# A four-layer graph network in one launch: layer 0's layernorm passes on GpSimd, its first row logits loaded early, layer 1's bias row added on VectorE

## The chip, the cores and the metric

The kernel runs on one core of a Trainium2 chip. The metric is the device time of one execution in microseconds (us). The kernel before takes 4507.97 us (median of three runs, 4505.92 to 4508.1); the profiled execution has a span of 4498.9 us from its first to its last instruction, and the profile's numbers are from that one.

A core has five engines with their own instruction streams, each working through its stream in order: TensorE (PE in the profile, and PEld for its weight loads), VectorE (DVE), ScalarE (ACT), GpSimd (POOL) and SyncE (SP, which here only issues transfers). They work in parallel and wait for one another by semaphores. Data moves between memory and the on-chip buffers by DMA.

## The reference

N is 4096 nodes, D is 256 features. Four layers follow one another, each with a residual and a layernorm:

```python
x = _layernorm(x + _L0_gnn_ref(x, W, b, a, adj))       # 8-head attention on the graph
x = _layernorm(x + _L1_gnn_ref(x, adj, weight, bias))  # (diag(adj) + adj) @ (x @ w) + bias
x = _layernorm(x + _L2_gnn_ref(x, adj, ...))           # top-p attention diffusion, two steps
x = _layernorm(x + _L3_gnn_ref(x, adj, W, b))          # mean aggregation, relu

def _L0_gnn_ref(x, W, b, a, adj_matrix):
    node_feats = (x @ W.T + b).reshape(num_nodes, num_heads, half)
    logit_parent = (node_feats * a[None, :, :half]).sum(axis=-1)
    logit_child = (node_feats * a[None, :, half:]).sum(axis=-1)
    attn_logits = leaky_relu(logit_parent[:, None, :] + logit_child[None, :, :], 0.2)
    attn_logits = where(abs(adj_matrix)[..., None] != 0.0, attn_logits, 0.0)
    attn_probs = softmax(attn_logits, axis=1)
    return einsum('ijh,jhc->ihc', attn_probs, node_feats)

def _L1_gnn_ref(x, adj, weight, bias):
    support = x @ weight
    return (diagonal(adj) + adj) @ support + bias      # the diagonal is added to every row
```

(The bodies of layers 2 and 3 are left out: the change does not touch them.)

## The kernel before

Layer 0 has two stages. `sums0` computes the node features and logits and, by dense matmuls over the whole adjacency, the sums that do not depend on the sign of a logit; it also writes a one-byte copy of the adjacency (`nad`), the row logits (`lpd`), the sums (`zd`) and the matmul operands (`gmd`) to memory. Then `layer0` goes through two halves of four heads each, and in each half through four tiles of 1024 rows. For each head it makes masks (logit sum above zero, and an edge), 32 column blocks of them in groups of four, partly on VectorE and partly on ScalarE, and multiplies them with `gm`. In half 1 it adds the residual and normalises.

```python
def moments(self, pool, src):                                   # cut
    for q in range(n):
        nc.vector.bn_stats(stats[:, q, :], src[:, q, :])        # L80
        nc.vector.bn_aggr(mv[:, q, :], stats[:, q, :])          # L81
    var = pool.tile([P, n], F32, name="ln_var")
    nc.gpsimd.tensor_scalar_add(var, mv[:, :, 1], EPS)          # L83
    nc.gpsimd.tensor_tensor(rstd, var, self.power..., ALU.pow)  # L84
    return mv, rstd

def layernorm(self, pool, dst, src):
    mv, rstd = self.moments(pool, src)
    for q in range(src.shape[1]):                               # L91
        self.nc.vector.tensor_scalar(dst[:, q, :], src[:, q, :], mv[:, q, 0:1], rstd[:, q:q + 1],
                                     op0=ALU.subtract, op1=ALU.mult)

def layer0(self):                                               # cut; Q = 8, NB = 32, K = 4, H = 8
    ...
    self.sums0(both, nlc, fac, lpd, nad, zd, gmd)
    self.open_x()
    self.load1()                                                # layer 1's weight and bias, on ScalarE's queue
    ...
    work = ctx.enter_context(tc.tile_pool(name="l0w", bufs=2))
    for half in range(2):
        for it in range(N // IT):
            i0 = it * Q
            ...                                                 # loads of na, and of gm at it == 0
            if half:
                nc.sync.dma_start(X[:, i0:i0 + Q, :], xr[:, i0:i0 + Q, :])
                y0 = work.tile([P, Q, D // 2], F32, name="y0", bufs=1)
                nc.sync.dma_start(y0, yd[i0:i0 + Q].rearrange("b p d -> p b d"))
            y = work.tile([P, Q, H // 2, C], F32, name="y")
            for hh in range(H // 2):
                h = half * (H // 2) + hh
                lpb = work.tile([P, IT], F32, name="lpb")
                nc.gpsimd.dma_start(lpb, bass.AP(tensor=lpd.tensor, ...))          # L243
                z = work.tile([P, Q, C1], F32, name="z")
                nc.gpsimd.dma_start(z, zd[i0:i0 + Q, :, h]...)                     # L246
                for g in range(NB // K):
                    ...
                    if g % 8 in (2, 5, 7):
                        for k in range(K):                                         # L257
                            nc.vector.tensor_scalar(sg[:, k, :], lpb, nlc[:, jc, h:h + 1], 2.0 ** -5, ...)
                        nc.vector.tensor_tensor(*bits, ALU.bitwise_and)            # L259
                    else:
                        for k in range(K):                                         # L264
                            nc.scalar.activation(sg[:, k, :], lpb, AF.Sign, scale=-1.0, ...)
                        nc.vector.scalar_tensor_tensor(bits[0], bits[1], ...)      # L266
                    ...                                                            # 32 matmuls, L272
                ...                                       # reduction of acc (L277), scaling, y of this head
            if not half:
                nc.gpsimd.dma_start(yd[i0:i0 + Q]..., y)
                continue
            for q in range(0, Q, 2):
                xs = X[:, i0 + q:i0 + q + 2, :]
                nc.vector.tensor_add(xs[:, :, :D // 2], xs[:, :, :D // 2], y0[:, q:q + 2])   # L296
                nc.vector.tensor_add(xs[:, :, D // 2:], xs[:, :, D // 2:], y[:, q:q + 2])    # L297
                self.layernorm(work, xs, xs)

def sums0(self, both, nlc, fac, lpd, nad, zd, gmd):             # cut
    ...                                                         # loads of w0, b0, a0
    for t, cs in ((w0, (0, 1)), (b0, (0,))):
        for c in cs:
            for s in range(2):
                prod = work.tile([P, H, C], F32, name="prod")
                nc.vector.tensor_mul(prod, t[:, c, :D]..., a_bc[:, s])                        # L375
                nc.vector.tensor_reduce(t[:, c, D + s * H:D + (s + 1) * H], prod, AX.X, ALU.add)  # L376
    ...                                                         # features and logits, support matmuls at L401
    self.factors0(wp, ps, both, nlc, fac)
    with nc.allow_non_contiguous_dma(reason="the diagonal"):
        nc.scalar.dma_start(self.diag, bass.AP(tensor=self.adjt.tensor, ...))                 # L432
    ...                                                         # the dense sums, matmuls at L479

def layer1(self):                                               # cut
    dg = pool.tile([P, NB], F32R, name="dg")
    nc.vector.tensor_copy(dg, self.diag)                        # L665
    ...                                                         # x @ w1, split into two parts, in XD
    ...                                                         # row = diagonal @ support + bias
    for b in range(NB):
        ps = psum.tile([P, 512], F32, name="ps_adj")            # psum has bufs=2
        ...                                                     # 32 matmuls into ps, L695
        xb = X[:, b:b + 1, :]
        nc.gpsimd.tensor_add(xb[:, 0], xb[:, 0], row)           # L700
        nc.vector.tensor_add(xb[:, 0], xb[:, 0], ps[:, :D])     # L701
        nc.vector.tensor_add(xb[:, 0], xb[:, 0], ps[:, D:])     # L702
        self.layernorm(work, xb, xb)
```

A tile scheduler sets the order of the instructions on each engine within a priority that follows the program, so instructions of a later part can be issued among those of an earlier one.

Of the kernel before, what the change touches and what calls it, by code (L numbers as in the profile page):

```python
# [9 lines left out]
F32 = mybir.dt.float32  # L10
I32 = mybir.dt.int32
F32R = mybir.dt.float32r
# [5 lines left out]
ALU = mybir.AluOpType  # L18
# [4 lines left out]
P = 128  # L23
# [28 lines left out]
class Net:  # L52
# [9 lines left out]
    def constants(self):  # L62
        nc = self.nc
        pool = self.ctx.enter_context(self.tc.tile_pool(name="const", bufs=1))
        self.ident = pool.tile([P, P], F32, name="ident")
        make_identity(nc, self.ident)
        self.power = pool.tile([P, 1], F32, name="power")
        nc.vector.memset(self.power, -0.5)
        self.deg = pool.tile([P, self.NB], F32, name="deg")
        self.diag = pool.tile([P, self.NB], F32, name="diag")  # L70

    def moments(self, pool, src):
# [13 lines left out]

    def layernorm(self, pool, dst, src):

        mv, rstd = self.moments(pool, src)
        for q in range(src.shape[1]):  # L90
            self.nc.vector.tensor_scalar(dst[:, q, :], src[:, q, :], mv[:, q, 0:1], rstd[:, q:q + 1],  # L91
                                         op0=ALU.subtract, op1=ALU.mult)

# [99 lines left out]
    def layer0(self):  # L193
        nc, tc, NB, D, N = self.nc, self.tc, self.NB, self.D, self.N
        H, C = 8, 32
        C1 = C + 1
        IT = min(1024, N)
        Q = IT // P
        keep = self.ctx.enter_context(tc.tile_pool(name="l0k", bufs=1, space=DRAM))
        self.fits = keep.tile([1, 1], I32, name="fits")  # L200
        with ExitStack() as ctx:
            pool = ctx.enter_context(tc.tile_pool(name="l0", bufs=1))
            dram = ctx.enter_context(tc.tile_pool(name="l0d", bufs=1, space=DRAM))

            both = pool.tile([P, NB, 2, H], F32, name="both")
            lp, lc = both[:, :, 0, :], both[:, :, 1, :]
            nlc = pool.tile([P, NB, H], F32, name="nlc")

            fac = pool.tile([P, 4, NB, H], F32, name="fac")
            lpd = dram.tile([H, N], F32, name="lpd")  # L210


            nad = self.nad
            zd = dram.tile([NB, P, H, C1], F32, name="zd")
            yd = dram.tile([NB, P, D // 2], F32, name="yd")
            gmd = dram.tile([2, P, NB, H // 2, 6 * C1], BF16, name="gmd")
            self.sums0(both, nlc, fac, lpd, nad, zd, gmd)

# [7 lines left out]
            gm = gp.tile([P, NB, H // 2, 6 * C1], BF16, name="gm")  # L226
            na = gp.tile([P, NB, IT], U8, name="na")
            for half in range(2):
                for it in range(N // IT):
# [10 lines left out]
                    for hh in range(H // 2):  # L240
                        h = half * (H // 2) + hh
                        lpb = work.tile([P, IT], F32, name="lpb")
                        nc.gpsimd.dma_start(lpb, bass.AP(tensor=lpd.tensor, offset=lpd.offset + h * N + it * IT,  # L243
                                                         ap=[[0, P], [1, IT]]))
                        z = work.tile([P, Q, C1], F32, name="z")
# [41 lines left out]
                        nc.vector.reciprocal(r, t1[:, :, C])  # L287
                        nc.vector.tensor_mul(y[:, :, hh, :], t1[:, :, :C], r.unsqueeze(2).to_broadcast([P, Q, C]))
                    y = y.rearrange("p q h c -> p q (h c)")
                    if not half:  # L290
                        nc.gpsimd.dma_start(yd[i0:i0 + Q].rearrange("b p d -> p b d"), y)
                        continue

                    for q in range(0, Q, 2):
                        xs = X[:, i0 + q:i0 + q + 2, :]
                        nc.vector.tensor_add(xs[:, :, :D // 2], xs[:, :, :D // 2], y0[:, q:q + 2])  # L296
                        nc.vector.tensor_add(xs[:, :, D // 2:], xs[:, :, D // 2:], y[:, q:q + 2])  # L297
                        self.layernorm(work, xs, xs)

# [47 lines left out]

    def sums0(self, both, nlc, fac, lpd, nad, zd, gmd):

# [5 lines left out]
        with ExitStack() as ctx:  # L355
# [15 lines left out]
            for t, cs in ((w0, (0, 1)), (b0, (0,))):  # L371
                for c in cs:
                    for s in range(2):
                        prod = work.tile([P, H, C], F32, name="prod")
                        nc.vector.tensor_mul(prod, t[:, c, :D].rearrange("p (h c) -> p h c", h=H), a_bc[:, s])  # L375
                        nc.vector.tensor_reduce(t[:, c, D + s * H:D + (s + 1) * H], prod, AX.X, ALU.add)  # L376
# [51 lines left out]
            nc.scalar.copy(total, pt[:, :W])  # L428
            self.factors0(wp, ps, both, nlc, fac)

            with nc.allow_non_contiguous_dma(reason="the diagonal"):
# [5 lines left out]
            nc.scalar.activation(elc, both[:, :, 1, :], AF.Exp)  # L437
            psz = ctx.enter_context(tc.tile_pool(name="l0apz", bufs=4, space=PSUM))

            def factored(b):  # L440
# [219 lines left out]
    def layer1(self):  # L660
        nc, tc, NB, D, X = self.nc, self.tc, self.NB, self.D, self.X
        with self.ctx1 as ctx:
            pool, w1, bias = self.pool1, self.weight1, self.bias1
            dg = pool.tile([P, NB], F32R, name="dg")
            nc.vector.tensor_copy(dg, self.diag)  # L665
            work = ctx.enter_context(tc.tile_pool(name="l1w", bufs=2))
# [20 lines left out]
            for b in range(NB):  # L687
# [11 lines left out]
                xb = X[:, b:b + 1, :]  # L699
                nc.gpsimd.tensor_add(xb[:, 0], xb[:, 0], row)  # L700
                nc.vector.tensor_add(xb[:, 0], xb[:, 0], ps[:, :D])  # L701
                nc.vector.tensor_add(xb[:, 0], xb[:, 0], ps[:, D:])  # L702
                self.layernorm(work, xb, xb)

# [766 lines left out]
```

## Time and profile before

| | before |
|---|---|
| median of three runs | 4507.97 us |
| span of the profiled execution | 4498.9 us |
| TensorE busy | 94% |
| VectorE busy | 74% |
| ScalarE busy | 61% |
| GpSimd busy | 7% |
| mean granted TensorE clock | 0.979 |

The profile is read in three ways below. The table of stages gives, for stretches of the span, how long each engine was busy in them. The timeline lists instructions in order of their start: start in us, duration in us, engine, line of the program, operation, output and inputs with their sizes, how many like instructions are put together, and in square brackets how long the engine had idled before it and what it had waited for. Engine names with a q are the sequencers that issue transfers. Idle time of an engine that does not set the end costs nothing.

### The profile page before, as it was taken

The numbers are of one execution on the slowest core, as the hardware profiler recorded it, in microseconds if no ns is written. First come the engines' busy times: TensorE is split into PE (matmuls) and PEld (weight loads), VectorE is DVE, ScalarE is ACT, GpSimd is POOL, SyncE is SP. The second block draws the span as 40 slices with busy tenths as digits, with TensorE's granted clock in tenths as the row PEclk, the third lists the DMA queues.
The fourth block names the chain that finished last, engine by engine and source line by source line (L and its number), as shares of the span: only waits on it lengthen the run. The fifth ranks groups of instructions, "written<-read, shape, count | busy, mean of one in ns | idle before, by whom it ended". The sixth has DMA issues, their size and how long they took to land. (4 is left out here: it accounts for less than half of the span.)

```text
span 4498.9 us, 70573 instructions
## 1 busy us (share of the span) xinstructions
PE 4245.9 (94%) x25625; PEld 3417.3 (76%) x25625; DVE 3342.9 (74%) x7657; ACT 2758.4 (61%) x5501; POOL 313.6 (7%) x538
## 2 busy tenths in 40 slices
PE   8999989999987999999999999887999999999799
PEld 7999989999986876677777767665666666666587
DVE  7632259999994447977777777388989999989354
ACT  5533369998873235866666666257677777676232
POOL 0111100001102100000000000001000000000011
PEclk9999999999998999999999999999999999999899
DMA  4655553332215964022222222530122222222541
GB/s 132 226 198 178 176 201 106 97 139 64 88 37 206 385 235 139 27 78 85 81 79 80 79 81 84 200 118 30 39 78 77 80 79 80 68 70 76 189 143 48
DMA packets 277781, 523.51 MB, mean 116 GB/s; under 512 B 36774, under 2 KB 112294, under 8 KB 273318
## 3 DMA queue, kind: packets, MB, share of 16 engines
q1 hardware_dynamic: 179268, 356.20, 23.2%
q10 hardware_dynamic: 85282, 122.62, 8.0%
q0 software_dynamic: 12864, 39.99, 2.9%
q8 instruction: 207, 3.39, 0.3%
q14 instruction: 160, 1.31, 0.1%
HBM read 363.63 MB, written 155.06 MB: 115 GB/s over the span
## 5 line engine op out<-in xcount | busy, mean ns | idle before, releaser
L1220 PE MATMUL ps_a<-X,aT 128*128 128x256 f32 x4096 | 965.1, 387 | 28.8 <-ACT aT L1217 28.7
L1220 PEld LDWEIGHTS ps_a<-X,aT 128*128 128x128 f32 x4096 | 763.8, 191 | 294.5 <-ACT aT L1217 135.2
L272 PE MATMUL acc<-gm,gt 128*128 128x198 bf16 x8192 | 709.4, 249 | 38.1 <-issue 18.1
L272 PEld LDWEIGHTS <-gt 128*128 128x128 fp8e4 x8192 | 703.9, 98 | 43.6 <-issue 18.3
L264 ACT ACTIVATE sg<-lpb,nlc 128x1024 fp8e4<-128x1024 f32 x640 | 670.5, 1135 | 78.5 <-DVE gt L266 38.1
L479 PE MATMUL pz<-src,ar 128*128 128x264 f32 x4096 | 510.7, 287 | 9.8 <-DVE ar L469 7.9
L159 PE MATMUL ps_r<-XD,adj_piece 128*128 128x512 f32 x2048 | 508.9, 400 | 10.0 <-DMA adj_piece<-adjs 9.5
L479 PEld LDWEIGHTS pz<-src,ar 128*128 128x128 f32 x4096 | 507.9, 190 | 12.6 <-DVE ar L469 9.7
L1217 ACT COPY aT<-ps_tp 128x512 f32<-128x512 f32 x512 | 277.5, 583 | 360.4 <-PE ps_tp L1215 355.9
L955 ACT ACTIVATE ja<-e,nc 128x2048 uint8<-128x2048 f32 x240 | 478.6, 1994 | 0.5 <-issue 0.2
L882 PE MATMUL ps_logit<-kT,q 64*128 64x512 f32 x1024 | 462.5, 637 | 4.0 <-ACT e L886 3.9
L159 PEld LDWEIGHTS ps_r<-XD,adj_piece 128*128 128x128 f32 x2048 | 382.7, 190 | 109.1 <-DMA adj_piece<-adjs 23.0
L901 DVE SCALAR_TENSOR_TENSOR v<-e,c 128x4096 bf16<-128x4096 f32 x100 | 447.2, 4472 | 7.2 <-ACT c L929 6.5
L1037 DVE MAX8 cand<-v 128x8 f32<-128x256 f32 x1024 | 360.7, 411 | 2.2
L1084 DVE SCALAR_TENSOR_TENSOR e<-e,edge 128x512 f32<-128x512 f32 x512 | 347.3, 745 | 1.5
L182 ACT ACTIVATE adj_piece<-na 128x1024 fp32r<-128x1024 fp8e4 x128 | 135.2, 1059 | 326.5 <-PE ps_adj L695 128.4
L472 ACT ACTIVATE nb<-a 128x512 uint8<-128x512 f32 x256 | 156.6, 630 | 289.2 <-DMA a<-in_adjt_dram 280.2
L1215 PE MATMUL ps_tp<-ident,e 128*128 128x128 f32 x2048 | 273.9, 275 | 38.9 <-DVE e L1084 26.1
L1033 DVE SCALAR_TENSOR_TENSOR v<-e,hi 128x2048 f32<-128x2048 f32 x128 | 300.9, 2351 | 1.7
L1215 PEld LDWEIGHTS ps_tp<-ident,e 128*128 128x128 f32 x2048 | 242.9, 142 | 77.5 <-DVE e L1084 29.5
L886 ACT ACTIVATE e<-ps_logit 128x1024 f32<-128x1024 f32 x256 | 261.0, 1020 | 50.1 <-PE ps_logit L882 35.4
L257 DVE TENSOR_SCALAR sg<-lpb,nlc 128x1024 fp8e4<-128x1024 f32 x384 | 273.9, 750 | 1.7
(301 smaller groups left out, 5076.7 us busy)
## 6 DMA issues: line engine op xcount, KB each, us to landing
adj_piece<-adjs SPq DMA_DIRECT2D x512, 256.0 KB
a<-in_adjt_dram SPq DMA_DIRECT2D x256, 256.0 KB
adjs<-adj_piece SPq DMA_DIRECT2D x128, 512.0 KB
na<-nad SPq DMA_DIRECT2D x64, 512.0 KB
na<-nad ACTq DMA_DIRECT2D x32, 1024.0 KB
nad<-nb POOLq DMA_DIRECT2D x128, 128.0 KB, 3.3
lpb<-lpd POOLq DMA_DIRECT2D x32, 512.0 KB, 4.1
xfd<-part ACTq DMA_DIRECT2D x63, 256.0 KB
```

Source lines behind the costliest of these rows:

```text
L159: nc.tensor.matmul(ps, a[:, k, :], rhs(jc).rearrange("p s d -> p (s d)"), start=(jc == 0 and own is None), stop=(jc == self.NB - 1))
L264: nc.scalar.activation(sg[:, k, :], lpb, AF.Sign, scale=-1.0, bias=nlc[:, jc, h:h + 1], saturate=False)
L272: nc.tensor.matmul(acc[:, q, :6 * C1], gt[:, k, q * P:(q + 1) * P], gm[:, jc, hh, :], start=(jc == 0 and q % 2 == 0), stop=(jc == NB - 1 a ...
L479: nc.tensor.matmul(pz[q][:, t, :W], ar[:, q, k, :], src[:, jc, t, s], start=(jc == 0 and s == 0), stop=(jc == NB - 1 and s == 1))
L882: nc.tensor.matmul(pl[:, s, :], q[s * A:(s + 1) * A, :], kT[s * A:(s + 1) * A, c * 512:(c + 1) * 512], start=True, stop=True)
L901: nc.vector.scalar_tensor_tensor(junk, e, c, e, op0=ALU.is_ge, op1=ALU.mult, accum_out=S)
L955: nc.scalar.activation(ja, e[:, s * HALF:(s + 1) * HALF], f, bias=nc1, accum_out=fs[:, i + s:i + s + 1])
L1033: nc.vector.scalar_tensor_tensor(v, ec, hi, ec, op0=ALU.is_lt, op1=ALU.mult, accum_out=sb[:, s:s + 1])
L1037: nc.vector.max(cand[:, 8 * j:8 * j + 8], v[:, k * 256:(k + 1) * 256])
L1084: nc.vector.scalar_tensor_tensor(ec, ec, edge[:, j:j + 1], ec, op0=ALU.is_ge, op1=ALU.mult)
L1215: nc.tensor.transpose(pt[:, k * P:(k + 1) * P], e[:, jc * P:(jc + 1) * P], self.ident)
L1220: nc.tensor.matmul(pa[:, :D], aT[:, k * P:(k + 1) * P], X[:, jc, :], start=(jc == 0), stop=(jc == NB - 1))
```

## The change

Four things change in the program:

1. In half 1 of layer 0, tiles 0 to 2: both residual adds and the normalise itself run on GpSimd, and each pair's layernorm is put off: it is queued in `later` and issued one pair after each of the following four heads. The last tile is as it was, on VectorE.
2. The first head's row logits have a tile of their own, `first`, which is loaded within `sums0`, right after the row logits are complete, so that the first masks need not wait for a load at the end of the dense sums. For the room, `prod` has one buffer instead of two.
3. The copy of the diagonal that layer 1's matmul needs (`dg`) is made in `sums0`, as `diagr`, and no longer at the head of layer 1.
4. In layer 1 the row is added on VectorE after the two sums, and no longer on GpSimd ahead of them.

```diff
         self.diag = pool.tile([P, self.NB], F32, name="diag")
+        self.diagr = pool.tile([P, self.NB], F32R, name="diagr")
...
-    def layernorm(self, pool, dst, src):
+    def layernorm(self, pool, dst, src, engine=None):
...
-            self.nc.vector.tensor_scalar(dst[:, q, :], ...
+            (engine or self.nc.vector).tensor_scalar(dst[:, q, :], ...
...
+            def row_logits(t, h, it):
+                nc.gpsimd.dma_start(t, bass.AP(tensor=lpd.tensor, offset=lpd.offset + h * N + it * IT, ap=[[0, P], [1, IT]]))
+                return t
+
+            first = pool.tile([P, IT], F32, name="lpb0")
...
-            self.sums0(both, nlc, fac, lpd, nad, zd, gmd)
+            self.sums0(both, nlc, fac, lpd, nad, zd, gmd, lambda: row_logits(first, 0, 0))
...
+            later = []
+            per_head = Q // 2 // (H // 2)
...
-                        lpb = work.tile([P, IT], F32, name="lpb")
-                        nc.gpsimd.dma_start(lpb, ...)
+                        lpb = row_logits(work.tile([P, IT], F32, name="lpb"), h, it) if h or it else first
...
+                        for xs in later[:per_head]:
+                            self.layernorm(work, xs, xs, nc.gpsimd)
+                        del later[:per_head]
...
+                    engine = nc.vector if i0 + Q == NB else nc.gpsimd
                     for q in range(0, Q, 2):
                         xs = X[:, i0 + q:i0 + q + 2, :]
-                        nc.vector.tensor_add(xs[:, :, :D // 2], xs[:, :, :D // 2], y0[:, q:q + 2])
-                        nc.vector.tensor_add(xs[:, :, D // 2:], xs[:, :, D // 2:], y[:, q:q + 2])
-                        self.layernorm(work, xs, xs)
+                        engine.tensor_add(xs[:, :, :D // 2], xs[:, :, :D // 2], y0[:, q:q + 2])
+                        engine.tensor_add(xs[:, :, D // 2:], xs[:, :, D // 2:], y[:, q:q + 2])
+                        if i0 + Q == NB:
+                            self.layernorm(work, xs, xs)
+                        else:
+                            later.append(xs)
...
-                        prod = work.tile([P, H, C], F32, name="prod")
+                        prod = work.tile([P, H, C], F32, name="prod", bufs=1)
...
             self.factors0(wp, ps, both, nlc, fac)
+            then()
...
+            nc.vector.tensor_copy(self.diagr, self.diag)
...
-            pool, w1, bias = self.pool1, self.weight1, self.bias1
-            dg = pool.tile([P, NB], F32R, name="dg")
-            nc.vector.tensor_copy(dg, self.diag)
+            pool, w1, bias, dg = self.pool1, self.weight1, self.bias1, self.diagr
...
-                nc.gpsimd.tensor_add(xb[:, 0], xb[:, 0], row)
                 nc.vector.tensor_add(xb[:, 0], xb[:, 0], ps[:, :D])
                 nc.vector.tensor_add(xb[:, 0], xb[:, 0], ps[:, D:])
+                nc.vector.tensor_add(xb[:, 0], xb[:, 0], row)
                 self.layernorm(work, xb, xb)
```

The changed kernel was built before the prediction, so the order of its instructions on each engine could be compared with that of the kernel before.

More of the change, by code (lines that the diff above doesn't have):

```diff
@@ L85, in moments @@
         return mv, rstd
-    def layernorm(self, pool, dst, src):
+    def layernorm(self, pool, dst, src, engine=None):
         mv, rstd = self.moments(pool, src)
         for q in range(src.shape[1]):
-            self.nc.vector.tensor_scalar(dst[:, q, :], src[:, q, :], mv[:, q, 0:1], rstd[:, q:q + 1],
-                                         op0=ALU.subtract, op1=ALU.mult)
+            (engine or self.nc.vector).tensor_scalar(dst[:, q, :], src[:, q, :], mv[:, q, 0:1], rstd[:, q:q + 1],
+                                                     op0=ALU.subtract, op1=ALU.mult)
     def transposed(self, psum, pool, src, name, bufs=2, out=None):
@@ L241, in layer0 @@
                         h = half * (H // 2) + hh
-                        lpb = work.tile([P, IT], F32, name="lpb")
-                        nc.gpsimd.dma_start(lpb, bass.AP(tensor=lpd.tensor, offset=lpd.offset + h * N + it * IT,
-                                                         ap=[[0, P], [1, IT]]))
+                        lpb = row_logits(work.tile([P, IT], F32, name="lpb"), h, it) if h or it else first
                         z = work.tile([P, Q, C1], F32, name="z")
@@ L346, in factors0, with sums0 @@
         nc.scalar.dma_start(self.fits, fits)
-    def sums0(self, both, nlc, fac, lpd, nad, zd, gmd):
+    def sums0(self, both, nlc, fac, lpd, nad, zd, gmd, then):
         nc, tc, NB, D, N = self.nc, self.tc, self.NB, self.D, self.N
```

## The prediction

> **What bounds the kernel now.** I read the totals first, then a table of busy time by stage, then the timeline around each place the diff touches.
>
> ```profile
> PE 4245.9 (94%) x25625; PEld 3417.3 (76%) x25625; DVE 3342.9 (74%) x7657; ACT 2758.4 (61%) x5501; POOL 313.6 (7%) x538
> ```
>
> TensorE (PE) is busy 94% of the span, so this change can win only where PE stands still: 4498.9 − 4245.9 = 253 us in all. The stage table (window in us, its length, busy PE, PEld, DVE, ACT and POOL, granted clock, DMA share, GB/s) says where. I set the borders by the lines that run: start, layer 0's dense sums, the step to the heads, half 0 and half 1 of the heads, into layer 1, layer 1, layers 2 and 3.
>
> ```profile
> 0.00:76.00 76.00, 57.75 (x291) 45.01 (x291) 55.92 (x128) 42.75 (x94) 5.86 (x26) 0.97 0.38 101
> ...
> 597.00:642.00 45.00, 27.51 (x304) 26.78 (x305) 24.74 (x32) 33.13 (x32) 3.47 (x5) 0.81 1.00 365
> 642.00:1016.00 374.00, 371.39 (x4355) 370.24 (x4353) 363.87 (x463) 357.99 (x343) 28.40 (x38) 1.00 0.33 108
> 1016.00:1344.00 328.00, 310.54 (x3539) 306.89 (x3536) 305.08 (x439) 279.35 (x267) 33.74 (x49) 0.97 0.21 65
> 1344.00:1420.00 76.00, 56.20 (x265) 45.63 (x266) 29.15 (x73) 25.71 (x54) 3.79 (x8) 0.87 0.51 195
> 1420.00:1445.00 25.00, 14.96 (x61) 11.96 (x61) 16.36 (x13) 2.12 (x2) 22.13 (x33) 0.83 0.20 81
> 1445.00:1655.00 210.00, 210.00 (x924) 173.72 (x922) 95.16 (x215) 64.93 (x75) 25.39 (x62) 1.00 0.86 340
> 1655.00:4499.00 2844.00, 2686.85 (x11800) 1929.26 (x11798) 2238.25 (x5852) 1747.86 (x4295) 97.49 (x194) 0.98 0.27 88
> ```
>
> From 1655 on, 63% of the span, the instruction order of every engine is the same in both kernels: nothing changes there. In half 0 (642 to 1016) PE, DVE and ACT are all 96 to 99% busy, a balance; in half 1 PE idles 17.5 us of 328, and in 1420 to 1445 it idles 10 of 25.
>
> The 32 head steps show by the starts of the reduction of `acc`: one head takes 20.98 us; the first head of each later row tile in half 0 and the first of half 1 takes 23.9 to 24.6. In half 1 the four heads after a tile's layernorms take 28.42 + 22.13 + 24.96 + 21.37 = 96.9 us where a group before them takes 3 × 20.97 + 24.59 = 87.5: 9.4 us too much, three times. The timeline at the first of those clusters:
>
> ```profile
> 1163.16 0.75 DVE L297 TENSOR_TENSOR X<-X,y 128x256 f32<-128x256 f32 x2
> ...
> 1166.20 0.73 DVE L91 TENSOR_SCALAR X<-X,ln_mv,ln_rstd 128x256 f32<-128x256 f32 x2 [0.84 <-POOL ln_rstd L84]
> ...
> 1171.32 4.27 ACT L264 ACTIVATE sg<-lpb,nlc 128x1024 fp8e4<-128x1024 f32 x4 [5.24 <-DVE gt L266]
> ...
> 1171.34 5.46 PE L272 MATMUL acc<-gm,gt 128*128 128x198 bf16 x32 [4.07 <-DVE gt L266]
> ```
>
> DVE works through adds, statistics and normalises, waits for the rstd each time, and PE and ACT starve (4.07, 5.24) for the mask words that DVE makes. The smaller excess comes from this line, once per tile:
>
> ```profile
> 815.23 1.43 DVE L296 TENSOR_TENSOR X<-X,y 128x256 f32<-128x256 f32 x4 [1.44 <-DMA y<-yd]
> ```
>
> Layer 1's pause:
>
> ```profile
> 1430.69 10.97 POOL L700 TENSOR_TENSOR X<-X,row 128x256 f32<-128x256 f32 x16
> 1430.75 11.05 DVE L91 TENSOR_SCALAR X<-X,ln_mv,ln_rstd 128x256 f32<-128x256 f32 x1 [6.21 <-POOL ln_rstd L84]
> ...
> 1442.73 32.57 PE L695 MATMUL ps_adj<-XD,adj_piece 128*128 128x512 f32 x134 [10.04 <-DVE X L702]
> ```
>
> A normalise that takes 0.41 us elsewhere took 11.05 while GpSimd (POOL) ran 16 row adds back to back; the two `ps` banks stayed full, and PE stood 10.04 us. Last, the step to the heads:
>
> ```profile
> 607.88 0.18 DVE L665 CAST dg<-diag 128x32 fp32r<-128x32 f32 x1 [9.58 <-DMA zd<-zt]
> 607.98 0.75 DVE L257 TENSOR_SCALAR sg<-lpb,nlc 128x1024 fp8e4<-128x1024 f32 x1
> 608.87 11.54 ACT L264 ACTIVATE sg<-lpb,nlc 128x1024 fp8e4<-128x1024 f32 x11 [23.15 <-DVE sg L257]
> ...
> 614.49 5.73 PE L272 MATMUL acc<-gm,gt 128*128 128x198 bf16 x49 [18.12 <-issue]
> ```
>
> **What the Trainium skill says.** "SBUF — State Buffer", § Who interferes with whom: VectorE and GpSimd share a port pair under an exclusive lock; tensor_scalar in a two-port mode and operations with two SBUF inputs contend, and the other side "fully blocks". The 11.05 us normalise agrees. Milder cases in layer 1 give a size: beside row adds a normalise took 0.81 instead of 0.41, an `adj_piece` conversion 1.22 and 0.88 instead of 0.69. I take 0.2 to 0.5 us per meeting. "GPSIMD Engine Reference", § 3.1 Elementwise — side-by-side cycle accounting, gives about 2.6 cycles an element with two inputs, an estimated 0.55 us for 256 elements before dispatch; the trace has 0.73 (median of 32). "DMA: Bandwidth & Descriptors", § Why small descriptors are slow (HBM only), lets one expect the diagonal's load, 4,096 pieces of four bytes, to be slow: it is issued at 4.85 us and its last completion in the trace is at 15.3, ten us for 16 KB.
>
> **A. Start, +3.8.** The built order puts the `diagr` copy eighth on VectorE, behind two of the four `w0` products. In-order VectorE must then wait for the diagonal until about 15.3. In the kernel before it finished `w` at 13.56 and PE began the support matmuls at 14.06. Afterwards: 15.3 + the copy 0.2 + two products and two reductions at 0.33 to 0.42, with conversions of 0.6 between, gives `w` at about 17 to 18.1, so PE slips 3 to 4 us. The sums behind it are PE-bound (510.7 of 521), so this is not caught up. +3.8, range +2 to +5.
>
> **B. Step to the heads, −2.5.** VectorE no longer waits for `dg`, and the first masks wait for `first` alone, which came long before. But ScalarE does only three masks before it issues layer 1's weight load, which still waits for a transfer that ended at 607.8. Three masks of 1.04 us are the head start, so about 3 of the 18.12 us come back, less a little, since the stage runs with DMA at 100% and `gm` and `na` arrive in pieces. −2.5, range −4 to −1.
>
> **C. The residual's first half, −4.** Three of four sets of y0 adds leave VectorE for GpSimd; the fourth stays. Each is worth 3.6 us of PE at most (24.6 − 20.98), three are 10.8. Against that: four GpSimd adds of 0.73 beside a VectorE that is 97% busy meet it four times, 4 × 0.35 = 1.4 us, and VectorE no longer waits for `y0`. (3.6 − 1.4) × 3 = 6.6; I take −4, as GpSimd's own late loads can delay a head. Range −8 to +2.
>
> **D. The layernorm clusters, −8.** Of the 10.9 us of VectorE work and wait in one cluster (4 adds and 8 normalises at 0.33, 8 statistics at 0.33, 8 aggregates at 0.1, waits 0.84 + 3 × 0.90), adds, normalises and rstd waits leave. The 3.44 us of statistics stay. And the order does not spread them: all four pairs' statistics stand within the first head of the next tile; the aggregates of pairs 2 and 3 wait for GpSimd's normalises of pairs 0 and 1 (two buffers of `ln_mv`), and the first statistics wait for GpSimd's adds. Contention: four adds and eight normalises at some 0.3 are 3.8; waits about 1. 3.44 + 3.8 + 1 − 1.5 that the heads' slack absorbs = 6.7 against 9.4: −2.7 a cluster, −8 for three. The last cluster stays as it is. Range −18 to +6.
>
> **E. Layer 1's pause, −10.** The row add on VectorE costs 0.42 a block; a block takes PE 7.25 us, and VectorE is busy 95 of 210 there. So the 10.04 us go, range −11 to −8. **F.** One add more stands after the last block's matmuls: +0.5.
>
> **Sum.** 3.8 − 2.5 − 4 − 8 − 10 + 0.5 = −20.2. 4507.97 − 20.2 ≈ 4487 us (−0.45%).
>
> **Rivals.** (1) The port lock eats the head stage's gain: GpSimd's twelve passes a tile each block VectorE's masks (0.69 us, tensor_scalar) or its two-input mask ANDs (1.22), and in a stage with three balanced engines each blocked us is PE time. For it: the 11.05 us line. Against: that was a queue of 16 with nothing between; here GpSimd waits for statistics between pairs. C and D then come to +8: 4508 us. (2) Full hiding: statistics too vanish in slack, and C and D give −9 and −27: about 4463 us. Against it: DVE 363.9 of 374 in half 0, no slack to hide in. (3) The step is bound by the arrival of `gm` and `na` (DMA share 1.00), and the start's wait is longer: B 0, A +5, so 4491 us. (4) Layer 1 becomes bound by DMA once the pause is gone (385 GB/s and 97% share from 1445 to 1550): E −5, 4492 us.
>
> **Range and chances.** C and D carry most of the doubt, some ±12; A, B and E ±3 together: 4470 to 4500 holds 8 in 10. A 2% gain needs 90 us, more than all the idle PE time the change touches (about 18 + 17.5 + 10 us and the tile steps' 15), a 2% loss something not seen. Faster 0.01, same 0.97, slower 0.02.
>
> **What would show it.** A: the first support matmul at about 18 instead of 14.06, behind a VectorE wait for the diagonal. B: first head matmul about 15 us after the last of the sums instead of 18.12. C and D: heads 4, 8 and 12 below 24, groups after the clusters about 94 us, and mask instructions longer than 0.69 or 1.22 beside GpSimd's adds. E: no PE gap of 10 us at the start of layer 1. Wrong would be: groups above 97 us, PE gaps behind statistics that wait for GpSimd, or a changed time after the layer-1 stage.

## The result, and the profile after

The changed kernel takes 4481.62 us (median of four runs, 4478.71 to 4483.64) against 4506.94 us of the kernel before: ratio 0.9945, 95% interval 0.9928 to 0.9963, or about 25 us less. The interval makes it 17 to 32 us. The prediction was 4487 with a range of 4470 to 4500. The profiled spans differ by 21.9 us (4498.9 and 4477.0). Line numbers in the changed kernel are some higher: the head matmuls L272 became L280, VectorE's masks L257 became L265, the sign masks' AND L266 became L274, layer 1's matmuls L695 became L711.

The totals of the changed kernel's page, same columns as before:

```profile
PE 4236.7 (95%) x25625; PEld 3409.6 (76%) x25625; DVE 3339.2 (75%) x7641; ACT 2759.6 (62%) x5501; POOL 387.2 (9%) x554
```

VectorE's busy time fell by 3.7 us only, and GpSimd's rose by 73.6. PE works 9.2 us less for the same 25,625 matmuls: they ran faster. Both come back below.

The table of busy time by stage of the changed kernel, now with its borders at the first and last matmul of each stage (window, length, PE, PEld, DVE, ACT, POOL, clock, DMA share, GB/s): start, dense sums, step to the heads, the heads in two parts, into layer 1, layer 1, the rest.

```profile
0.00:78.60 78.60, 57.74 (x292) 44.38 (x292) 56.50 (x129) 43.30 (x94) 6.39 (x27) 0.99 0.38 104
78.60:601.00 522.40, 510.00 (x4096) 506.56 (x4096) 214.00 (x446) 203.60 (x344) 93.70 (x124) 0.99 0.59 189
601.00:615.70 14.70, 0.00 (x0) 0.00 (x0) 3.88 (x8) 5.80 (x6) 2.94 (x4) 0.57 0.91 319
615.70:990.00 374.30, 372.38 (x4344) 371.17 (x4345) 359.85 (x444) 362.77 (x347) 41.06 (x48) 0.99 0.42 136
990.00:1331.10 341.10, 332.25 (x3851) 329.60 (x3848) 323.82 (x433) 302.74 (x289) 117.22 (x87) 0.99 0.21 64
1331.10:1358.80 27.70, 8.29 (x41) 6.99 (x41) 13.67 (x39) 3.82 (x9) 3.81 (x8) 0.63 0.28 92
1358.80:1630.30 271.50, 270.50 (x1211) 222.50 (x1209) 128.33 (x294) 89.70 (x124) 24.34 (x62) 1.00 0.79 316
1630.30:4477.00 2846.70, 2685.56 (x11798) 1928.41 (x11798) 2239.12 (x5853) 1747.85 (x4293) 97.79 (x194) 0.98 0.27 88
```

With the same borders in the kernel before (first and last matmul of each stage) the time went here:

| stretch, us | before | after | difference |
|---|---|---|---|
| start to the first dense sum | 76.2 | 78.6 | +2.4 |
| dense sums | 520.2 | 522.4 | +2.2 |
| last dense sum to first head matmul | 18.1 | 14.7 | −3.4 |
| 32 heads | 729.4 | 715.4 | −14.0 |
| last head to layer 1's adjacency | 27.8 | 27.7 | −0.1 |
| layer 1's adjacency matmuls | 283.6 | 271.5 | −12.1 |
| the rest | 2843.7 | 2846.7 | +3.0 |

The heads are counted better by PE than by the reductions that I used in the prediction. The trace has all 8192 head matmuls, so every 256th is the start of a head on PE. An undisturbed head is then 21.76 us, a group of four 87.1. The groups of four (half 0, then half 1) are, in us:

| kernel | group 1 | 2 | 3 | 4 | 5 | 6 | 7 | 8 |
|---|---|---|---|---|---|---|---|---|
| before | 90.4 | 88.8 | 87.5 | 87.1 | 87.2 | 95.3 | 96.1 | 97.0 |
| after | 91.7 | 87.1 | 87.2 | 87.2 | 87.1 | 89.9 | 92.5 | 92.7 |

Groups 6 to 8 follow the three tiles whose layernorms moved. They lose 13.3 of the heads' 14.0 us. The timeline at the first of these clusters in the changed kernel (start, duration, engine, line, operation, idle before and releaser):

```profile
1065.22 5.11 POOL L309 TENSOR_TENSOR X<-X,y 128x256 f32<-128x256 f32 x4 [1.11 <-DVE y L296]
...
1073.81 4.92 POOL L92 TENSOR_SCALAR X<-X,ln_mv,ln_rstd 128x256 f32<-128x256 f32 x2
...
1078.77 0.18 DVE L82 BATCH_NORM_AGGREGATE ln_mv<-ln_stats 128x2 f32<-128x6 f32 x1 [1.04 <-POOL X L92]
...
1082.31 0.25 DVE L82 BATCH_NORM_AGGREGATE ln_mv<-ln_stats 128x2 f32<-128x6 f32 x2 [2.33 <-POOL X L92]
...
1088.66 2.19 ACT L272 ACTIVATE sg<-lpb,nlc 128x1024 fp8e4<-128x1024 f32 x2 [5.42 <-DVE gt L274]
1088.69 1.54 PE L280 MATMUL acc<-gm,gt 128*128 128x198 bf16 x16 [2.06 <-DVE gt L274]
```

The waits for rstd on VectorE are gone. In their place are two waits of an aggregate for GpSimd's normalise of an earlier pair (1.04 and 2.33), and PE still starves, but for 0.24 and 2.06 us. At the first cluster the kernel before had:

```profile
1074.49 4.55 PE L272 MATMUL acc<-gm,gt 128*128 128x198 bf16 x32 [2.53 <-DVE gt L266]
1081.01 86.26 PE L272 MATMUL acc<-gm,gt 128*128 128x198 bf16 x992 [1.97 <-DVE gt L259]
```

The prediction takes its lines from 1163.16 on for the first cluster; they are of the second, where PE stood 4.07 and 1.05 us, and in the changed kernel 2.80 and 0.41. A pair of normalises took 4.92 us on GpSimd here; on VectorE two took 0.73 before.

The step to the heads in the changed kernel:

```profile
601.90 1.15 ACT L272 ACTIVATE sg<-lpb,nlc 128x1024 fp8e4<-128x1024 f32 x1 [11.73 <-DVE zt L505]
...
603.33 2.19 ACT L272 ACTIVATE sg<-lpb,nlc 128x1024 fp8e4<-128x1024 f32 x2 [0.29 <-issue]
...
612.26 0.41 ACTq L111 DMA_DIRECT2D w<-in_w_dram  x1
613.24 17.78 ACT L272 ACTIVATE sg<-lpb,nlc 128x1024 fp8e4<-128x1024 f32 x17 [7.72 <-issue]
614.42 1.23 DVE L274 SCALAR_TENSOR_TENSOR gt<-sg,na 128x1024 uint32<-128x1024 uint32 x1 [10.68 <-ACT sg L272]
...
615.75 15.81 PE L280 MATMUL acc<-gm,gt 128*128 128x198 bf16 x160 [14.75 <-issue]
...
635.15 1.23 DVE L267 TENSOR_TENSOR gt<-sg,na 128x1024 uint32<-128x1024 uint32 x1 [1.99 <-DMA na<-nad]
```

ScalarE makes three masks at once, from 601.9, then stands 7.72 us behind the issue of layer 1's weight load at 612.26, and only then makes the fourth that the first mask words need. A little later VectorE waits 1.99 us for `na`. The kernel before and l0_ln (below), without the early load, have no such wait, and first_diag, with it, has: part of the head start is lost to a load. The start and layer 1, same view, each in its own stretch of the span:

```profile
14.25 1.27 PE L416 MATMUL ps_nf<-w,xT 128*128 128x272 f32 x2 [6.61 <-ACT xT L412]
14.50 0.27 DVE L456 CAST diagr<-diag 128x32 fp32r<-128x32 f32 x1 [2.23 <-DMA diag<-in_adjt_dram]
...
17.39 3.99 PE L416 MATMUL ps_nf<-w,xT 128*128 128x272 f32 x8 [1.87 <-DVE w L391]
```

```profile
1406.59 33.75 PE L711 MATMUL ps_adj<-XD,adj_piece 128*128 128x512 f32 x148
...
1410.00 0.43 DVE L718 TENSOR_TENSOR X<-X,row 128x256 f32<-128x256 f32 x1
...
1412.85 0.41 DVE L92 TENSOR_SCALAR X<-X,ln_mv,ln_rstd 128x256 f32<-128x256 f32 x1 [1.16 <-POOL ln_rstd L85]
```

VectorE waits 2.23 us for the diagonal, and PE 1.87 for the second half of `w` behind it. In layer 1 the first normalise takes 0.41 us, and PE runs 148 matmuls in a row where the kernel before had the pause of 10.04.

### The profile page after: what moved, and what is told of

It is laid out like the page before. It is cut to its first block, busy times and chain, and to the rows that moved or that the text cites. A ratio compares the mean times of both kernels' runs of the same rounds, so it can differ in the third digit from the quotient of the medians.

```text
span 4477.0 us, 70563 instructions
## 1 busy us (share of the span) xinstructions
PE 4236.7 (95%) x25625; PEld 3409.6 (76%) x25625; DVE 3339.2 (75%) x7641; ACT 2759.6 (62%) x5501; POOL 387.2 (9%) x554
## 5 line engine op out<-in xcount | busy, mean ns | idle before, releaser
L280 PE MATMUL acc<-gm,gt 128*128 128x198 bf16 x8192 | 704.7, 248 | 25.5 <-issue 14.7
L280 PEld LDWEIGHTS <-gt 128*128 128x128 fp8e4 x8192 | 700.8, 97 | 29.4 <-issue 14.9
L272 ACT ACTIVATE sg<-lpb,nlc 128x1024 fp8e4<-128x1024 f32 x640 | 671.3, 1135 | 59.5 <-DVE gt L274 34.6
L497 PE MATMUL pz<-src,ar 128*128 128x264 f32 x4096 | 510.0, 287 | 12.8 <-DVE ar L487 10.6
L183 ACT ACTIVATE adj_piece<-na 128x1024 fp32r<-128x1024 fp8e4 x128 | 135.3, 1059 | 314.2 <-PE ps_adj L1393 95.3
L84 POOL TENSOR_SCALAR ln_var<-ln_mv 128x1 f32<-128x1 f32 (+1 forms) x144 | 60.4, 419 | 3040.0 <-DVE ln_mv L82 1384.2
```

The lines of the kernel that those rows point to most:

```text
L280: nc.tensor.matmul(acc[:, q, :6 * C1], gt[:, k, q * P:(q + 1) * P], gm[:, jc, hh, :], start=(jc == 0 and q % 2 == 0), stop=(jc == NB - 1 a ...
L497: nc.tensor.matmul(pz[q][:, t, :W], ar[:, q, k, :], src[:, jc, t, s], start=(jc == 0 and s == 0), stop=(jc == NB - 1 and s == 1))
```

## The experiments

All times are medians; each ratio is against runs of the kernel before on the same chip. It is not the quotient of the two medians: in l0_ln the medians differ by 11.7 us and the ratio makes it 16. Stage times are from the one profiled execution of each. First, how far such stage times scatter: the dense sums have the same matmuls in all fourteen profiles and took 519.7 to 525.4 us, the rest behind layer 1 2843.5 to 2853.0. The +2.2 and +3.0 in the table above lie within that and are not shown to be the change's. The changed kernel once more:

> The changed kernel once more, beside the runs that follow on the same chip. Theory (the 2.2 us of the dense sums and the 3 us behind layer 1 are scatter from run to run): first dense-sum matmul at 78.5, heads 715, layer 1 271.5 us again; the dense sums anywhere from 519 to 526 us and the rest from 2843 to 2853. Rival (they belong to the change): 522.4 and 2846.7 again, within 0.5 us. Time 24 to 26 us less than before.

4484.42 us, ratio 0.9955 (0.9941 to 0.9968): 18.6 us less than before by the medians, 20 by the ratio, and not the 24 to 26 expected. Start 78.7, dense sums 522.1, step 15.0, heads 717.4, layer 1 271.0, rest 2851.4. The rest moved by 4.7 us and the heads by 2.0 on the same program (group 8: 94.2 instead of 92.7), the start, the step and layer 1 by 0.5 at most. So the signs and sizes of the start, the step, the heads and layer 1 repeat (layer 1 took 270.9 to 274.0 in the ten profiles with the row added on VectorE); the rest is scatter. The dense sums' 522 came twice, but kernels with the same code in that stage have 519.7 (first_diag) and 520.1 (later_dve).

**Layer 1 alone.**

```diff
-                nc.gpsimd.tensor_add(xb[:, 0], xb[:, 0], row)
                 nc.vector.tensor_add(xb[:, 0], xb[:, 0], ps[:, :D])
                 nc.vector.tensor_add(xb[:, 0], xb[:, 0], ps[:, D:])
+                nc.vector.tensor_add(xb[:, 0], xb[:, 0], row)
```

> The kernel before with part 4 alone (layer 1's row added on VectorE after the two sums). Theory (a queue of row adds on GpSimd locks VectorE out at the start of layer 1): 12 us less than before, the stage from the first to the last matmul into ps_adj goes from 283.2 to about 271 us, no PE gap of 10 us in it, the 32 heads stay at 729.4 us. Rival (the pause is only moved: once it is gone the loads and stores of that stage bind): at most 6 us less, and new PE gaps on DMA in layer 1.

4495.33 us, 9.7 less, ratio 0.9978 (0.9970 to 0.9986), which is 6 to 14 us. Layer 1's matmuls took 270.9 us, the heads 730.2. The table of that stage (window, length, busy PE, PEld, DVE, ACT, POOL, clock, DMA share, GB/s):

```profile
1374.00:1644.90 270.90, 270.14 (x1210) 222.49 (x1208) 128.24 (x294) 89.62 (x124) 24.26 (x62) 1.00 0.80 315
```

PE is busy for all but 0.8 us: transfers don't take the pause's place. The same add, left on GpSimd but behind the two sums:

```diff
-                nc.gpsimd.tensor_add(xb[:, 0], xb[:, 0], row)
                 nc.vector.tensor_add(xb[:, 0], xb[:, 0], ps[:, :D])
                 nc.vector.tensor_add(xb[:, 0], xb[:, 0], ps[:, D:])
+                nc.gpsimd.tensor_add(xb[:, 0], xb[:, 0], row)
```

> The kernel before, with layer 1's row add left on GpSimd but put behind the two sums, so that GpSimd can run only one a block. Theory (the harm was the queue of adds that ran ahead, not GpSimd as such): no 11 us normalise, no 10 us PE gap, 11 to 12 us less than before, adj stage about 271 us. Rival (any GpSimd add on X in that stage holds VectorE up): gain under 6 us and PE gaps in each block.

4495.94 us, ratio 0.9980 (0.9973 to 0.9987), layer 1 at 272.6 us, where the costliest groups have (busy us, mean ns, then idle before and releaser):

```profile
L695 PE MATMUL ps_adj<-XD,adj_piece 128*128 128x512 f32 x1024 | 236.1, 391 | 0.0
...
L702 POOL TENSOR_TENSOR X<-X,row 128x256 f32<-128x256 f32 x31 | 23.0, 741 | 198.7 <-DVE X L701 198.7
...
L80 DVE BATCH_NORM_STATS2 ln_stats<-X 128x6 f32<-128x256 f32 x31 | 13.2, 427 | 27.5 <-POOL X L702 27.5
```

GpSimd still makes every add, 0.74 us each, and VectorE's statistics now wait 27.5 us for them in all. PE doesn't care: its idle ahead of these matmuls is 0.0. So it was the queue of sixteen adds which could run ahead, and not GpSimd as the place of the add, that made the pause.

**Layer 0's layernorms alone** (part 1 of the diff put into the kernel before).

> The kernel before with part 1 alone (residual adds and normalise on GpSimd, put off). Theory (the gain in the heads comes from this part and needs no other): 13 to 14 us less than before; on PE the 32 heads take about 715 to 717 instead of 729.4 us, head groups 6, 7 and 8 some 90 to 93 instead of 95 to 97. Rival (GpSimd's passes take back what they save, the shorter head stage came from the earlier start): within 3 us of before. Layer 1 must keep its 10 us gap in both.

4493.28 us, 11.7 less, ratio 0.9964 (0.9951 to 0.9978). Heads 714.6 us, groups 6 to 8 90.4, 92.5, 92.6, layer 1 with its pause at 285.8. The theory holds: part 1 alone has the whole gain of the heads.

**The early load and the diagonal alone** (parts 2 and 3 in the kernel before).

> The kernel before with parts 2 and 3 alone (first row logits loaded early, diagonal copied in the dense sums). Theory (start loses what the step to the heads wins): first dense-sum matmul at 78.6 instead of 76.2, last dense sum to first head matmul 15 instead of 18.4 us, the second head about 1 us slower; sum between -1 and +3 us against before. Rival (the dense sums' own extra 2.2 us in the changed kernel belong to this part too): +2 to +4. Other rival (the head start is worth all of its 3.4 us): -2 or less.

4504.19 us, 0.8 less, ratio 0.9998 (0.9989 to 1.0006): no difference that the runs can tell. Start 78.5, dense sums 519.7, step 15.3: the start loses 2.3, the step wins 2.8, and group 1 of the heads gives back 1.3 (91.7 instead of 90.4). The dense sums did not grow, so their extra 2.2 shows no tie to this.

**The diagonal's copy later, in the changed kernel:**

```diff
-            nc.vector.tensor_copy(self.diagr, self.diag)
+            nc.vector.tensor_scalar(self.diagr, self.diag, total[:, C:C + 1], None, op0=ALU.min)
```

> The changed kernel, but the copy of the diagonal is min(diagonal, count of nodes), with the count taken from the column sums, so that VectorE can make it only once those are complete (same values). Theory (the start lost 2.4 us to the wait for the diagonal): first dense-sum matmul back at about 76.2, 2 to 3 us less than the changed kernel, 27 to 28 us less than before. Rival (the products would have been late anyway, by the single prod buffer): first dense-sum matmul stays at 78 or later, no gain.

4485.31 us, ratio 0.9952 (0.9938 to 0.9965). The start of the dense sums is back at 76.4, as the theory has it, and PE's first support matmuls run without the second wait. In the timeline of the start:

```profile
13.78 4.90 PE L416 MATMUL ps_nf<-w,xT 128*128 128x272 f32 x10 [6.05 <-ACT xT L412]
```

Yet the time is not below the changed kernel's. The profiled execution, the slowest of its five, has dense sums of 525.2 and a rest of 2853.0, both near the top of their scatter, but that explains this execution and not the median. The wait is shown; its worth in the total is not.

**Which of the moves earns the heads' gain.** First everything back on VectorE, but still put off behind the next heads:

```diff
-                            self.layernorm(work, xs, xs, nc.gpsimd)
+                            self.layernorm(work, xs, xs)
...
-                    engine = nc.vector if i0 + Q == NB else nc.gpsimd
+                    engine = nc.vector
```

> The changed kernel with everything of layer 0's layernorms back on VectorE, but still put off behind the following heads. Theory A (the gain of the head stage is mostly that VectorE's work moved to GpSimd): head groups 6, 7, 8 back to 94 to 97 us, 4 us or more slower than the changed kernel. Theory B (the gain is that VectorE no longer sits waiting for rstd at the seam, so putting off is enough): groups 89 to 93, no slower than the changed kernel. In both the y0 adds on VectorE cost half 0 at most 2 us.

4486.09 us, ratio 0.9962 (0.9949 to 0.9974); groups 6 to 8 at 92.6, 93.4, 95.2, between the two theories, and the heads at 724.9. Groups 2 to 4 took 264.3, 2.9 more than in l0_ln, a little over the 2 that I allowed. Then with the first of the two edits only, so that the adds stay on GpSimd:

> The changed kernel with the residual adds on GpSimd, but the put-off normalise on VectorE. The normalise took 2.1 us on GpSimd (0.41 on VectorE) and the statistics of pairs 2 and 3 waited 1.0 and 2.3 us for it. Theory (that wait and the lock cost more than the eight passes of 0.33 us do on VectorE): groups 6 to 8 about 90 us, 3 to 6 us less than the changed kernel. Rival (VectorE has no room, each pass on it costs PE): groups 94 us, 3 to 6 us slower.

4486.37 us, ratio 0.9962 (0.9951 to 0.9973); groups 6 to 8 at 91.8, 94.4, 94.6. My theory fell: taking the slow normalise off GpSimd did not win 3 to 6 us, the heads took 721.2 instead of 715.4. In the total time these two kernels can't be told from the changed one; the heads tell them apart. The group lines of the whole head stage tell the steps (busy us, mean ns, idle before, and what ended it). The kernel before:

```profile
L272 PE MATMUL acc<-gm,gt 128*128 128x198 bf16 x8192 | 709.4, 249 | 38.1 <-issue 18.1 <-DVE gt L266 12.7 <-DVE gt L259 7.1
...
L257 DVE TENSOR_SCALAR sg<-lpb,nlc 128x1024 fp8e4<-128x1024 f32 x384 | 273.9, 750 | 1.7
```

Put off, all on VectorE:

```profile
L280 PE MATMUL acc<-gm,gt 128*128 128x198 bf16 x8192 | 705.3, 249 | 34.4 <-DVE gt L274 15.5 <-issue 14.8 <-DVE gt L267 4.0
```

Put off, adds on GpSimd, normalise on VectorE:

```profile
L280 PE MATMUL acc<-gm,gt 128*128 128x198 bf16 x8192 | 705.2, 249 | 30.9 <-issue 15.0 <-DVE gt L274 12.0 <-DVE gt L267 3.5
```

The changed kernel:

```profile
L280 PE MATMUL acc<-gm,gt 128*128 128x198 bf16 x8192 | 704.7, 248 | 25.5 <-issue 14.7 <-DVE gt L267 7.7 <-DVE gt L274 3.0
...
L265 DVE TENSOR_SCALAR sg<-lpb,nlc 128x1024 fp8e4<-128x1024 f32 x384 | 282.8, 772 | 2.0
L274 DVE SCALAR_TENSOR_TENSOR gt<-sg,na 128x1024 uint32<-128x1024 uint32 x160 | 196.3, 1227 | 17.6 <-ACT sg L272 17.4
L92 POOL TENSOR_SCALAR X<-X,ln_mv,ln_rstd 128x256 f32<-128x256 f32 x24 | 50.3, 2104 | 1.3
```

The "issue" part is the step to the heads. What PE waited for mask words ("DVE gt") goes 19.8, 19.5, 15.5, 10.7 us down these four. Putting off alone takes no wait away; it cuts it into smaller pieces, and PE's busy time for the same 8192 matmuls drops from 709.4 to 705.3. The adds are then worth about 4 us of wait, the normalises 4.8, or 2.2 by the repeat of the changed kernel, which has 13.3 where it had 10.7. The normalises' part includes their waits: between 1040 and 1325 us VectorE stands 11.4 us for rstd with them on VectorE, and not at all with them on GpSimd. The price shows in VectorE's masks: 750 ns a piece before, 772 after, 22 ns × 384 = 8.5 us. Of the 384 masks, 42 overlap one of GpSimd's adds or normalises in the changed kernel; these take 0.94 us on average, the others 0.75, and the longest 1.23.

**Truly spread.** The built order of the changed kernel still has all four pairs' statistics in one head. To hold each pair behind its own head I let the statistics share one rotating buffer with the head's reciprocal `r`, so that they can't start before it is free:

```diff
-                        r = work.tile([P, Q], F32, name="r")
+                        r = work.tile([P, 12], F32, name="r", bufs=1)[:, :Q]
...
                         for xs in later[:per_head]:
-                            self.layernorm(work, xs, xs, nc.gpsimd)
+                            stats = work.tile([P, 12], F32, name="r", bufs=1)
+                            self.layernorm(work, xs, xs, nc.gpsimd, stats.rearrange("p (n k) -> p n k", n=2))
```

(`moments` takes the given `stats` instead of a tile of its own.)

> The changed kernel, but the statistics share one buffer with the heads' reciprocal, so that each pair's layernorm is truly held behind its own head, one pair a head. Theory (what is left of the clusters, 13.5 us over 3 x 87.2, comes from all four pairs standing in the first head): groups 6 to 8 about 88 to 89.5 us, 7 to 12 us less than the changed kernel, and no head of 24.6 or 27.2. Rival (the work costs the same wherever it stands, since VectorE is full in every head): groups 91 to 93 us with every head at 22.5 to 23.5, same time within 3 us.

4471.97 us, ratio 0.9926 (0.9909 to 0.9942). Groups 6 to 8 at 87.2, 87.5, 89.6 and the heads at 704.6: the rival fell, the work vanishes when it stands alone. But the stretch from the last head to layer 1 grew from 27.7 to 30.6. So each pair ahead of its head's `r` instead of behind it, with the loop over `later` moved up by those lines:

> The truly spread kernel, but each put-off pair stands ahead of its head's reciprocal and is so held behind the head before; the last pair no longer trails the last head. Theory (the spread run gave back 3 us between the last head and layer 1, 30.6 instead of 27.7, because the third tile's last pair came after the last head): that stretch back to 27.7, heads at 704 to 705, some 2 to 3 us less than the spread kernel, 34 to 36 less than before. Rival (the stretch is longer since the last tile's own layernorms come closer to the end of the heads): it stays at 30.6, same time.

4466.4 us, ratio 0.9917 (0.9904 to 0.9931), 36.6 us less than before and the lowest of all, though its interval overlaps that of the spread kernel. Groups 6 to 8 at 87.2, 87.2, 87.3, heads 702.0, and the stretch behind them 27.5, as the theory says. Its group lines:

```profile
L281 PE MATMUL acc<-gm,gt 128*128 128x198 bf16 x8192 | 700.8, 248 | 15.8 <-issue 14.6 <-DVE gt L268 1.1
...
L266 DVE TENSOR_SCALAR sg<-lpb,nlc 128x1024 fp8e4<-128x1024 f32 x384 | 283.0, 773 | 1.7
...
L93 POOL TENSOR_SCALAR X<-X,ln_mv,ln_rstd 128x256 f32<-128x256 f32 x24 | 81.6, 3405 | 1.3
```

The masks are as slow as in the changed kernel (773 ns), and the normalises slower still (3.4 us), but PE waits 1.1 us in 32 heads. With the diagonal's later copy added:

> spread_early with the copy of the diagonal tied to the column sums. Theory (the start's 2.2 us are worth having): 2 us less than spread_early. Rival (the dense sums wait for loads of the adjacency that come no earlier, so an earlier start is lost there; the diag_late run started 2.2 us earlier and ended the sums no sooner): end of the dense sums and time the same within 1 us.

4467.98 us, ratio 0.9921 (0.9908 to 0.9935). The start is 3.0 us earlier (76.3 against 79.3), the dense sums last the same (523.3 and 523.2), and the last adjacency matmul of layer 1 comes 1.7 us earlier, 1617.0 against 1618.7. That speaks against the rival (the dense sums did not eat the start), but the time doesn't show a gain: it stays open at 2 us. Last, the spread kernel with its normalise on VectorE:

> The truly spread kernel with the put-off normalise on VectorE (adds stay on GpSimd). Theory (with the work spread VectorE still has no room: 20.7 busy of 21.76 us a head, and it must wait 0.9 us for rstd each time): each head of groups 6 to 8 at 22.5 to 23.5 us, groups 90 to 93, 8 to 14 us slower than spread. Rival (spreading is all, the engine does not matter): groups 87 to 89, within 2 us of spread.

4482.18 us, ratio 0.9954 (0.9940 to 0.9968); groups 88.2, 95.4, 95.1, heads 719.1, single heads of up to 25.0. The group line:

```profile
L281 PE MATMUL acc<-gm,gt 128*128 128x198 bf16 x8192 | 702.9, 248 | 31.3 <-DVE gt L268 15.5 <-issue 15.1
```

The wait for mask words is back at 15.5. Spread, but with the normalise on VectorE, is worth no more than the changed kernel. Two things go with that move, the passes themselves and their waits: between 1040 and 1325 us VectorE stands 10.6 us for rstd, in the spread kernel not at all. No run sets them apart.

## Why the prediction was right, and where it was not

The time lay in the range. The sum, 20.2 (so 4487.8), was 5 us short of the 25 and close to the 19 to 20 of the repeat, so in total time no miss is shown; some of the terms were wrong both ways:

| step | predicted | measured in the profile | verdict |
|---|---|---|---|
| A, start | +3.8 | +2.4 | mechanism right; the diagonal was waited for only until 14.50, not 15.3, and the first support matmul came at 14.25, not at about 18: the third slipped, to 17.39 |
| B, step to the heads | −2.5 | −3.4, then +1.3 in group 1 | right: three masks, then 7.72 us behind the weight load's issue; the 1.3 goes with the wait for `na` |
| C, y0 adds in half 0 | −4 | −1.9 | wrong: nearly nothing was there to win |
| D, layernorm clusters | −8 | −13.3 (12.9 in l0_ln, 11.3 in the repeat) | mechanism right, one term missing |
| E, layer 1's pause | −10 | −12.1 | right, the same term missing |
| F, end of layer 1, and the rest | +0.5 | +3.0 | scatter, 2843.5 to 2853.0 |

**C** failed at "Each is worth 3.6 us of PE at most (24.6 − 20.98)". I took the starts of VectorE's reduction for heads. Three times 20.98 and one 24.59 are 87.5, but four heads of 21.76 on PE are 87.0: the reduction's place within a head shifts by 3 us over a tile, and PE hardly notices. On PE's own matmuls groups 2 to 4 held 263.4 us before, against 3 × 87.1 = 261.3. The loss was 2 us, and l0_ln, with 261.5, took it all.

**D**'s sum of VectorE's work was near the mark for PE's waits: "DVE gt" fell by 9.1 us (19.8 to 10.7) where C and D together promised 12, D alone 8. In groups 6 to 8 PE's pauses fell from 17.3 to 8.9 us. That this met the 8 is partly luck: I allowed 3.8 us of contention and 1 us of waits a cluster, and the masks beside GpSimd's passes lost some 2.6, while the first cluster's waits are 3.4 (1.04 + 2.33). What I left out is that a pause can make the matmuls after it slower. PE's busy time for the 8192 matmuls fell by 4.7 us (709.4 to 704.7), and 9.1 + 4.7 is the heads' 14 us. The granted clock shows it: 0.88 in the first head of the first cluster before (1057.4 to 1085.8), 1.00 in the same head after. Right behind pauses of the kernel before, and again a little later, PE did (same columns as in the tables by stage):

```profile
1171.34:1174.75 3.41, 3.41 (x21) 3.12 (x22) 2.56 (x8) 3.41 (x4) 1.00 (x3) 0.50 0.00 0
1177.86:1181.27 3.41, 3.41 (x40) 3.41 (x41) 3.41 (x4) 2.30 (x3) 0.00 (x0) 1.00 0.28 114
1442.74:1446.74 4.00, 4.00 (x10) 3.13 (x11) 2.62 (x5) 0.85 (x2) 3.39 (x6) 0.50 0.75 291
1446.74:1450.74 4.00, 4.00 (x19) 3.28 (x18) 2.92 (x8) 2.00 (x3) 1.78 (x3) 0.99 0.70 273
```

Half the clock is half the matmuls (21 and 40, 10 and 19). Not every pause does it: behind the one of 2.06 us in the changed kernel the clock stays at 1.00, and spread_dve, with 15.5 us of waits in pauses of 2.6 at most and a clock of 1.00, has 702.9 us of busy time. So it is not the sum of the waits that sets the price, and cutting pauses up, as putting off does, won 4.1 us where the waits stayed. Which pauses bring the half clock stays open.

**E** is the same: the 10.0 us of idle went, and the 1211 matmuls of the stage took 270.5 instead of 272.7 us, so 2.2 more. The clock from 1421 to 1445 was 0.82, and the last two lines above are the stretch behind the pause: 4 us at half the clock are 2 us lost. The three profiles with the pause have 272.7 to 273.7 us of busy time here, the ten with the row on VectorE 270.1 to 270.7.

Of the **rivals**, the contention of (1) is measured, 8.5 us more VectorE time in the masks, but it did not eat the gain: statistics, two waits and dearer masks together still left VectorE less in PE's way than adds, normalises and rstd waits had. The contention I allowed, 0.3 us for each of 12 passes a tile and 1.4 for a tile's y0 adds, is 15 for three tiles, and 8.5 were measured. Full hiding (2) was not what this change does, but it is what it was meant to do, and spread_early shows that it can be had: the reason I gave against it, VectorE at 364 of 374 us, was wrong as a limit. Statistics of 0.86 us a head, the prediction's 3.44 by four, fit into the 21.76 us of PE time; all four pairs in one head don't. The step bound by `gm` and `na` (3) came true in part: the step won 3.4 us, but VectorE then waited 1.99 for `na`, and group 1 gave 1.3 back. What did not happen is a layer 1 bound by DMA (4), whose PE idle is 1.0 of 271.5 us with all its transfers.

The Trainium skill's "SBUF — State Buffer", § Who interferes with whom, says that the order of issue decides who blocks. That fits: in layer 1 VectorE was held for 11 us, in the heads GpSimd is slowed most. Its normalise, 1.22 us at the shortest, took 2.10 on average in the changed kernel and 3.41 in spread_early. That this is the lock and not GpSimd's own speed was not tried apart.

## What to carry to other kernels

When work is to be spread over later steps, look at the built order whether it was: here all four pairs, ready at once, stood in the first head, and a shared buffer that ties each piece to its step made 18 us here against the changed kernel on the same chip (4466.4 and 4484.42). Count a stage in units of the engine that sets the end, here every 256th matmul; the period of another engine's instruction can wander by 3.6 us and mean nothing. A slow engine is a fine place for work that nobody waits for: with normalises of 3.0 us on GpSimd PE waited 3.1 us for mask words in 32 heads (spread); with them on VectorE, where waits for rstd come along, 15.5 (spread_dve).

## What the runs showed of the hardware

- A pause of PE can cost more than itself: the idle that went was 9.1 us in the heads and 10.0 in layer 1, and with it 4.7 and 2.2 us of busy time of the same matmuls. Behind pauses of 4.07 and 10.04 us the granted clock was 0.50, and PE did 21 and 10 matmuls where it did 40 and 19 at 1.00 and 0.99. Behind a pause of 2.06 us it was 1.00.
- A normalise of 128x256 (tensor_scalar with two per-partition operands) took 0.41 us on VectorE and 1.21 to 6.30 on GpSimd; the two-input add 0.74 in layer 1, and 1.16 to 1.71 (X += y) in the heads beside a busy VectorE.
- Stages with the same matmuls scatter: 519.7 to 525.4 us and 2843.5 to 2853.0 us over fourteen profiles, so that 2 us at the start could be seen in the trace and not in the time.
